# Projecting queries and keys without the heads' padding, and sending each head to its quarter by DMA

## The chip, the cores and the metric

The kernel runs on one core of a Trainium2 chip. The metric is the device time of one execution in microseconds (us). One core has TensorE (PE), VectorE (DVE), ScalarE (ACT), GpSimd (POOL) and SyncE (SP), each with its own queue of instructions in program order, and sixteen DMA engines. Transfers are issued by instructions on the queues of SP, ACT and POOL; "Lnnn" is a line of the kernel before.

## The reference

x has 4 batches of 512 tokens with 288 features; a condition of 4 x 288 steers the normalisations.

```python
mod = silu(c) @ w_adaln + b_adaln                  # six vectors of 288 for each batch
sh_msa, sc_msa, g_msa, sh_mlp, sc_mlp, g_mlp = split(mod, 6)
h = layernorm(x) * (1 + sc_msa) + sh_msa
q, k, v = heads(h @ w_qkv + b_qkv)                 # 16 heads of 18
o = softmax(q @ k.T * 18**-0.5) @ v                # per batch and head, 512 x 512
x = x + g_msa * (o @ w_proj + b_proj)
xn = layernorm(x) * (1 + sc_mlp) + sh_mlp
gates, idx = top2_softmax(xn @ w_gate)             # 4 experts, two for each token
moe = sum over the two experts e of gate * (gelu(xn @ w1[e] + b1[e]) @ w2[e] + b2[e])
x = x + g_mlp * moe                                # hidden size 1152
U = qr(P).Q                                        # 288 x 64
R = expm(A(silu(c) @ W.T + b))                     # one skew 64 x 64 matrix for each batch
out = x + ((x @ U) @ R - x @ U) @ U.T
```

All of it is float32.

## The kernel before

**Attention.** The four batches are done one after another. A batch is 4 groups g of 4 heads, a group 4 steps t of 128 keys: n = 4*b + g counts the groups, and a step (g, t) of a batch does the scores z of 4 heads (L1678: eight matmuls into two z tiles), two exps on ScalarE into es (L1687) and, one step later, the products av of es and the values vt (L1696). In the tiles each head has 32 partitions, of which 18 are used, so that z and av can take a quarter of TensorE's array for each head. The values of a batch are products pv of the transposed, modulated rows hT (L1625); VectorE adds the bias bv on the way to vt (L1632).

**Queries and keys.** The padding of a head to 32 lies already in the weights: wqk holds 4 groups x 128 columns, with zeros in the rest of each head's 32. `project(n)` makes two products for group n, one for the queries and one for the keys. Each is three matmuls (the 288 features in three chunks of 96 rows) into a bank pq, and ScalarE adds the bias on the way from pq to the group's tile qk (L1662), of which there are two by turns. No transfer is needed. There are 16 groups and so 32 products. The products of batch 0's first group stand ahead of the loop; those of group n+1 are done in the steps (g, 0) or (3, 1) and (g, 2) of group n.

**The division.** `normalize(n)` copies a group's av to oraw (ScalarE, L1715). Row 18 of each head's 32 holds the sums of the weights; four DMAs on SP's queue bring them to den (L1718), VectorE takes the reciprocals (L1724), four more bring them back into rr (L1728), and in the next group VectorE spreads them over the heads' rows as rd (L1735) and multiplies into oT (L1736). `merge` then projects oT (po, L1752) and adds the result to x (og, L1761; POOL's xs, L1762).

**What lies in the steps besides.** The code gives each step a list of pieces, in an order written by hand: `also((g, t), piece)` puts a piece at its end, and `beside` holds a queue of pieces of which each step takes one. Such pieces are:
- the modulation for the later stages (`pr`, L1200, with the weights wadb; modrows; POOL's pairs mdr, gates and modrow, L1213 and L1214), and behind it on POOL's queue the loads of the rotation's weights wr, whose results go through a DRAM tile udr (L1266, a row of stores on SP's queue) into the matrices of the exponential (pf, pw, L1335 to L1364);
- the columns of the QR (L1480 to L1525, a chain of small VectorE instructions for each of 64 columns);
- the routing of the batch before: the logits, the top two, the ranks and at last `where` (L2005), the slot of each token and expert for batches 0 and 1;
- POOL's scatters of the normalised rows into those slots (L2008): each step takes one or two from a list, 16 of them in batch 3, and the load xg of the first expert's slots is on POOL's queue behind the last of them (L2051 to L2056). TensorE's transposes for the first expert wait for xg.

**After the attention** come the experts (ph, L2296; pe, L2356) and the rotation, on which TensorE is busy to the end.

**Ahead of the loop** VectorE clears one vt (L1045, 128x2048), POOL clears the other and some constants, the first rows xs are normalised (rs on POOL, xh on VectorE), transposed (L1143), and the first products and values follow. On SP's queue stand the loads of wada, x, wqk (in two pairs), wadb and the rest; on ScalarE's those of badT, bqk, wv and bv.

**Banks.** The products pq, pv, pr, po and the transposes share three PSUM banks (`bank`), z has two tiles of two banks, av one. hT has one buffer.

Of the kernel before, what the change touches and what calls it, by code (L numbers as in the profile page):

```python
# [10 lines left out]
F32 = mybir.dt.float32  # L11
I32 = mybir.dt.int32
AF = mybir.ActivationFunctionType
# [5 lines left out]
P = 128  # L19
# [794 lines left out]
def fast_path(  # L814
# [123 lines left out]
    def bank(shape, name):  # L938

        banks[0] += 1  # L940
        if third and banks[0] % 3 == 0:
            return third[0].tile(shape, F32, tag="n", name=name)
        return ps_m.tile(shape, F32, tag="m", name=name)
# [10 lines left out]
    with ExitStack() as s1:  # L954
# [14 lines left out]
        nc.sync.dma_start(out=wada, in_=wad[:, :, : 2 * C])  # L969
        badT = const.tile([CC, 6, NK], F32, name="badT")  # L970
        nc.scalar.dma_start(out=badT, in_=b_adalnT)
        bqk = const.tile([P, 2, NG], F32, name="bqk")
        nc.scalar.dma_start(out=bqk, in_=b_qk)
        for t in range(NT):
            nc.sync.dma_start(out=xs[:, t, :], in_=x[0, ts(t, P), :])

# [2 lines left out]
        nc.gpsimd.memset(scp, 0.0)  # L979
        sc = scp[:, :, :B]  # L980
        nc.scalar.activation(sc, cs, AF.Silu)
        wqk = wat.tile([CC, NK, 2, NG * P], F32, name="wqk")
        wqv = w_qk.rearrange("(k p) t f -> p k t f", p=CC)
        for i in range(2):
            nc.sync.dma_start(out=wqk[:, :, i, :P], in_=wqv[:, :, i, :P])
        wv = wat.tile([CC, NK, C], F32, name="wv")
        nc.scalar.dma_start(out=wv, in_=w_v.rearrange("(k p) f -> p k f", p=CC))
        bv = const.tile([P, C], F32, name="bv")
        nc.scalar.dma_start(out=bv, in_=b_v.partition_broadcast(P))
        for i in range(2):  # L990
            nc.sync.dma_start(out=wqk[:, :, i, P:], in_=wqv[:, :, i, P:])
        wadb = ada.tile([CC, NK, 4 * C], F32, name="wadb")
        nc.sync.dma_start(out=wadb, in_=wad[:, :, 2 * C :])
        badr = ada.tile([P, C], F32, name="badr")
        nc.gpsimd.memset(badr, 0.0)
        for i in range(4):
            nc.sync.dma_start(
                out=badr[i * HQ : i * HQ + B, :],
                in_=b_adaln[ds((2 + i) * C, C)].partition_broadcast(B),
            )  # L1000
        pt = rot.tile([D, C], F32, name="pt")
        nc.sync.dma_start(out=pt, in_=pT)
        for b in range(1, B):
            nc.sync.dma_start(
                out=xs[:, b * NT : (b + 1) * NT, :],
                in_=x[b].rearrange("(t p) c -> p t c", p=P),
            )
        bp = const.tile([P, C], F32, name="bp")
        nc.sync.dma_start(out=bp, in_=b_proj.partition_broadcast(P))
        wgT = const.tile([CC, NK, E], F32, name="wgT")  # L1010
        nc.sync.dma_start(out=wgT, in_=w_gate)
        b1s = const.tile([P, E, NF], F32, name="b1s")
        nc.sync.dma_start(out=b1s, in_=b1T)
        nc.sync.dma_start(out=wp, in_=w_proj.rearrange("g p c -> p g c"))

        def shift_scale(between):
            pm = bank([P, 2, NK, B], "pm")
# [122 lines left out]
        def modulate_T(b, which, xh, k, dst):  # L1140
            pt = bank([P, N], f"pt{which}{b}{k}")
            for t in range(NT):
                nc.tensor.transpose(  # L1143
                    pt[:CC, ts(t, P)], xh[:, t, ds(k * CC, CC)], ident
                )
            nc.scalar.activation(
                dst[:, k, :],
                pt[:CC, :],
                AF.Identity,
                bias=modT[:, 2 * which, k, b : b + 1],  # L1150
                scale=modT[:, 2 * which + 1, k, b : b + 1],
            )
# [36 lines left out]
        def other_modulation():  # L1189

            rows = ada.tile([P, C], F32, name="modrows")
            mdr = dram.tile([4, B, C], F32, name="mdr")
            to = (gates[:, 0], modrow[:, 0], modrow[:, 1], gates[:, 1])

            def product():

                pr = bank([P, N], "pr")
                for k in range(NK):
                    for i in range(4):
                        nc.tensor.matmul(  # L1200
                            pr[ts(i, HQ), :C],
                            scp[:, k, :],
                            wadb[:, k, ts(i, C)],
                            start=(k == 0),
                            stop=(k == NK - 1),
                        )
                nc.vector.tensor_add(rows, pr[:, :C], badr)
                one = rows[2 * HQ : 3 * HQ, :]
                nc.vector.tensor_scalar_add(one, one, 1.0)

            def spread():
                for i in range(4):
                    nc.gpsimd.dma_start(out=mdr[i], in_=rows[i * HQ : i * HQ + B, :])  # L1213
                    nc.gpsimd.dma_start(out=to[i], in_=mdr[i].partition_broadcast(P))  # L1214

            return [product, spread]

        def skew_matrices(between):
# [7 lines left out]
            udr = dram.tile([D, B, D], F32, name="udr")  # L1226
            wr = skew.tile([CC, NK, NV], F32, name="wr")
            brs = skew.tile([P, width], F32, name="brs")
            row = skew.tile([P, width], F32, name="row")

            def loads():
                for i in range(4):
# [373 lines left out]
                + [half, whole],  # L1606
            )

        hTs, oTs, qks, avs, xhs = {}, {}, {}, {}, {}
        
        def begin(b):


            xhs[b] = statistics(b, 0)
            hT = a2.tile([CC, NK, N], F32, tag="hT", name=f"hT{b}", bufs=1)
            hTs[b] = hT
            vt = vts[b % 2]

            def norm():
                xhs[b] = normalized(b, 0, *xhs[b])  # L1620

            def values(t):
                pv = bank([P, C], f"pv{b}{t}")
                for k in range(NK):
                    nc.tensor.matmul(  # L1625
                        pv,
                        hT[:, k, ts(t, P)],
                        wv[:, k, :],
                        start=(k == 0),
                        stop=(k == NK - 1),  # L1630
                    )
                nc.vector.tensor_tensor(  # L1632
                    vt[:, t, :, 0:HD],
                    pv.rearrange("p (h d) -> p h d", d=HD),
                    bv.rearrange("p (h d) -> p h d", d=HD),
                    ALU.add,
                )

            return (
                norm,  # L1640
                [lambda k=k: modulate_T(b, 0, xhs[b], k, hT) for k in range(NK)],
                [lambda t=t: values(t) for t in range(NT)],
            )

        def project(n):

            b, g = divmod(n, NG)
            qk = a2.tile([P, 2, N], F32, tag="qk", name=f"qk{n}")
            qks[n] = qk

            def product(i):
                hT = hTs[b]
                pq = bank([P, N], f"pq{n}{i}")
                for k in range(NK):
                    nc.tensor.matmul(  # L1655
                        pq,
                        wqk[:, k, i, ts(g, P)],
                        hT[:, k, :],
                        start=(k == 0),
                        stop=(k == NK - 1),  # L1660
                    )
                nc.scalar.activation(  # L1662
                    qk[:, i, :], pq, AF.Identity, bias=bqk[:, i, g : g + 1]
                )

            return [lambda i=i: product(i) for i in range(2)]

        def weigh(n, t):  # L1670


            qk, es = qks[n], []
            zs = [
                ps_s.tile([P, 2, N], F32, tag="z", name=f"z{n}{t}{i}") for i in range(2)
            ]
            for c in range(4):
                nc.tensor.matmul(  # L1678
                    zs[c // 2][:, c % 2, :],
                    qk[ts(c, HQ), 1, ts(t, P)],  # L1680
                    qk[ts(c, HQ), 0, :],
                    start=True,
                    stop=True,
                )
            for i, z in enumerate(zs):
                e = ex.tile([P, 2, N], F32, tag="es", name=f"es{n}{t}{i}")
                nc.scalar.activation(e, z, AF.Exp, scale=SCALE)  # L1687
                es.append(e)
            return es
# [14 lines left out]
        def normalize(n):  # L1704
# [26 lines left out]
                    )  # L1731

            def divide():
                rd = rt.tile([P, N], F32, tag="rd", name=f"rd{n}")
                nc.vector.stream_shuffle(rd, rr, [HD] * HQ)  # L1735
                nc.vector.tensor_mul(oTs[b][:, g, :], oraw, rd)  # L1736

            return first, reciprocals, divide

# [293 lines left out]
        NN = B * NG  # L2033
        norm, turns, values = begin(0)
        shift_scale(norm)
        for piece in turns + project(0) + values:
            piece()
        ST = CAPS[0] // P
        NB = 2
# [132 lines left out]
        for n in range(NN):  # L2172
            b, g = divmod(n, NG)
            if g == 0:
# [19 lines left out]
                for step in ((0, 0), (0, 1), (0, 3), (3, 1)):  # L2194
                    also(step, column)
                also((2, 3), lambda b=b: residual(b))
            if n + 1 < NN:
                query, key = project(n + 1)
                steps[g, int(g == 3)].insert(0, query)
                steps[g, 2].append(key)  # L2200
            if n == NN - 1:
                wx = wxs[0]
                weights = [expert_weights(0)]
# [464 lines left out]
```

## Time and profile before

| | us |
|---|---|
| median of 3 runs (732.49 to 734.12) | 732.83 |
| the profiled execution | 733.85 |
| its span in the profile | 732.1 |
| first z of batch 0, 1, 2, 3 | 26.68, 98.88, 180.64, 263.92 |
| first ph of the experts | 338.24 |

The profile comes from one execution, and its times count from the start of the span. In a row of groups stand the line, the engine, the operation, out<-in with the shapes and the number of instructions, then the busy time and the mean duration in ns of one, then the engine's idle time before them and what ended most of it. A row of the timeline has the start, the busy time, the engine, line and instructions, and in brackets the idle time ahead of it and its releaser; consecutive instructions of one kind are put together (x8). A window row gives, for a stretch of time, the busy time of each engine and in brackets its number of instructions, then the granted TensorE clock, the share of the DMA engines and GB/s. A line of the waits has the total, the number of waits and the longest.

### The profile page before, as it was taken

The page shows a single profiled execution, that of the slowest core. Times are in us where ns is not written, and L with a number is a line of the kernel's source. Part 1 is how long each engine was busy: PE and PEld are TensorE (multiplying, and loading weights), DVE is VectorE, ACT ScalarE, POOL GpSimd, SP SyncE. Part 2 cuts the span into 40 slices and gives each one's busy share as a digit, 9 for nine tenths or more (in the row PEclk, how much of TensorE's full clock was granted, in tenths as well). Part 3 has the DMA queues.
Part 4 walks back from the last instruction along what each step waited for, and adds up shares of the span by engine and source line. Part 5 has one row for each costly group of instructions (what it writes and reads, how often), then busy time and mean ns, then how long its engine had stood idle before and what let it go on. Part 6 is the DMA issues. An engine that isn't in the chain of part 4 may idle for free. (4 is left out here: it accounts for less than half of the span.)

```text
span 732.1 us, 11398 instructions
## 1 busy us (share of the span) xinstructions
PE 704.6 (96%) x3627; PEld 404.2 (55%) x3627; DVE 509.2 (70%) x2237; ACT 278.5 (38%) x427; POOL 216.9 (30%) x311
## 2 busy tenths in 40 slices
PE   6999999999999999998999999999999999999995
PEld 5432334334353444324677776777667776676763
DVE  3565678796887879685268888888888886004335
ACT  2455554454525543474222423223233232221232
POOL 4035900620026013761047064441203123031110
PEclk9999999999999999999999999999999999999998
DMA  9547700000000001144252252365324153205044
GB/s 228 149 132 196 271 3 6 1 2 2 2 1 1 3 18 60 35 147 93 61 171 70 78 179 80 131 166 165 83 77 140 28 170 78 81 29 187 37 137 146
DMA packets 65511, 66.69 MB, mean 91 GB/s; under 512 B 31625, under 2 KB 55982, under 8 KB 65441
## 3 DMA queue, kind: packets, MB, share of 16 engines
q1 hardware_dynamic: 57376, 42.48, 21.0%
q0 software_dynamic: 7360, 22.91, 9.7%
q10 hardware_dynamic: 704, 0.49, 0.3%
q8 instruction: 30, 0.49, 0.3%
q14 instruction: 41, 0.33, 0.2%
HBM read 48.08 MB, written 18.09 MB: 90 GB/s over the span
## 5 line engine op out<-in xcount | busy, mean ns | idle before, releaser
L2356 PE MATMUL pe<-w2s,hm 128*128 128x288 f32 (+1 forms) x648 | 163.7, 408 | 0.0
L1687 ACT ACTIVATE es<-z 128x1024 f32<-128x1024 f32 x128 | 124.2, 1021 | 84.6 <-PE z L1678 84.0
L2296 PE MATMUL ph<-xgT,w1s 128*128 128x288 f32 (+2 forms) x576 | 151.8, 413 | 0.4
L2356 PEld LDWEIGHTS pe<-w2s,hm 128*128 128x128 f32 (+1 forms) x648 | 118.7, 187 | 31.5 <-issue 2.3
L2296 PEld LDWEIGHTS ph<-xgT,w1s 128*128 128x128 f32 x576 | 105.8, 190 | 40.2 <-issue 11.2
L2318 ACT ACTIVATE hm<-ph,b1r 128x576 f32<-128x576 f32 (+2 forms) x72 | 49.8, 737 | 131.1 <-PE ph L2309 121.2
L1678 PE MATMUL z<-qk 32*128 32x512 f32 x512 | 90.0, 640 | 3.0 <-ACT es L1687 2.8
L1655 PE MATMUL pq<-hT,wqk 96*128 96x512 f32 x192 | 90.7, 609 | 0.0
L1696 PE MATMUL av<-es,vt 128*32 128x512 f32 x512 | 69.1, 612 | 0.0
L1655 PEld LDWEIGHTS pq<-hT,wqk 96*128 96x128 f32 x192 | 34.3, 191 | 54.1 <-issue 39.4
L2371 POOL TENSOR_TENSOR y<-y,gb 128x288 f32<-128x288 f32 x32 | 27.3, 854 | 117.6 <-ACT y L2370 117.5
L2008 POOL DMA_INDIRECT slots<-xr,where x32 | 32.0, 1001 | 92.3 <-DVE where L2005 48.6
L2370 ACT ACTIVATE y<-pe,weight 128x288 f32<-128x288 f32 x32 | 16.0, 500 | 104.8 <-PE pe L2356 104.5
L2372 POOL DMA_INDIRECT chosen<-y,place x36 | 36.6, 1017 | 57.2 <-DVE y L2368 35.0
L1678 PEld LDWEIGHTS z<-qk 32*128 32x128 f32 x512 | 25.8, 182 | 48.4 <-ACT es L1687 30.7
L1762 POOL TENSOR_TENSOR xs<-xs,og 128x288 f32<-128x288 f32 x16 | 12.6, 801 | 125.8 <-DVE og L1761 125.8
L1478 DVE SCALAR_TENSOR_TENSOR q<-q 64x1 f32<-64x1 f32 (+1 forms) x192 | 44.2, 230 | 7.0
L1662 ACT ACTIVATE qk<-pq,bqk 128x512 f32<-128x512 f32 x32 | 22.0, 687 | 69.8 <-PE pq L1655 69.8
L1489 DVE STREAM_SHUFFLE wj<-pt 32x288 f32<-32x288 f32 (+47 forms) x96 | 42.1, 439 | 0.7
L1696 PEld LDWEIGHTS av<-es,vt 128*32 128x32 f32 x512 | 10.1, 108 | 48.1 <-issue 42.7
L1752 PE MATMUL po<-wp,oT 128*128 128x288 f32 x128 | 33.8, 412 | 1.2 <-DVE oT L1736 0.7
L1460 DVE SCALAR_TENSOR_TENSOR pt<-wj,uf,pt 64x288 f32<-64x288 f32 (+62 forms) x63 | 32.6, 517 | 2.2
(273 smaller groups left out, 901.5 us busy)
## 6 DMA issues: line engine op xcount, KB each, us to landing
w2s<-in_w_dram SPq DMA_DIRECT2D x8, 1296.0 KB
w1s<-in_w_dram SPq DMA_DIRECT2D x8, 1152.0 KB
slots<-empty POOLq DMA_DIRECT2D x36, 148.0 KB
yc<-chosen SPq DMA_DIRECT2D x4, 576.0 KB
out_dram<-xs SPq DMA_DIRECT2D x8, 288.0 KB
wr<-in_wrT_dram POOLq DMA_DIRECT2D x4, 567.0 KB
xg<-slots SPq DMA_DIRECT2D x4, 512.0 KB
xg<-slots SPq DMA_DIRECT2D x3, 640.0 KB
```

The source lines that it names most:

```text
L1460: nc.vector.scalar_tensor_tensor(m, w, u[rows, :], m, ALU.mult, ALU.add)
L1478: nc.vector.scalar_tensor_tensor(s, u, part, s, ALU.mult, ALU.add)
L1489: nc.vector.stream_shuffle(wj[o : o + HQ, j:], pt[o0 : o0 + HQ, j:], [j % HQ] * HQ)
L1655: nc.tensor.matmul(pq, wqk[:, k, i, ts(g, P)], hT[:, k, :], start=(k == 0), stop=(k == NK - 1),)
L1678: nc.tensor.matmul(zs[c // 2][:, c % 2, :], qk[ts(c, HQ), 1, ts(t, P)], qk[ts(c, HQ), 0, :], start=True, stop=True,)
L1687: nc.scalar.activation(e, z, AF.Exp, scale=SCALE)
L1696: nc.tensor.matmul(avs[n][ts(c, HQ), :], vts[b % 2][:, t, 4 * g + c, :], es[c // 2][:, c % 2, :], start=(t == 0), stop=(t == NT - 1),)
L1752: nc.tensor.matmul(po, oTs[b][:, g, ts(t, P)], wp[:, g, :], start=(g == 0), stop=(g == NG - 1),)
L2296: nc.tensor.matmul(ph[:, j, :SB], w1s[:, k, ts(f, P)], xgT[:, k, ts(j, SB)], start=(k == 0), stop=False,)
L2318: nc.scalar.activation(hm[:, f, : CAPS[r]].rearrange("p (j s) -> p j s", j=NB), ph[:, :, :SB], AF.Gelu_apprx_tanh, bias=b1r[:, h, r, f : f ...
L2356: nc.tensor.matmul(po[ts(m, rows), :], slots_[:, f, :], w[:, f, :], start=(f == 0), stop=(f == NF - 1),)
L2372: nc.gpsimd.indirect_dma_start(out=chosen[h], out_offset=bass.IndirectOffsetOnAxis(ap=place[:, t : t + 1], axis=0), in_=y, in_offset=None, ...
```

## The change

The padding is taken out of the products. The 16 heads are cut into 7 + 7 + 2: `parts_of` gives five items, the queries and the keys of heads 0 to 6 (126 columns each), of heads 7 to 13 (126 each), and queries and keys of heads 14 and 15 together (72). A batch thus has 5 products, where it had 8. `compact` builds the weights without padding from the loaded ones, on ScalarE: one large copy and some copies of a single row for each item. The row is the bias: the weights get a 97th row in their first chunk, hT a 97th row of ones, so that the eviction is a copy. The values get their bias in the same way, and their eviction moves from VectorE to ScalarE.

The result of a product is not where z reads it: a head's 18 rows must be at its quarter. So the evictions go to `row` (one buffer) or `last`, and `send` brings each head from there to the tile of its group by a DMA on ScalarE's queue: one of 18x1024 for q and k of a head, for heads 14 and 15 two of 18x512. That is 18 transfers for a batch. The four qk tiles now live as long as the kernel; VectorE clears them once (128x1024 each), since only 18 of each 32 rows are ever written.

The order: heads 0 to 6 of batch 0 are projected and sent ahead of the loop, before the values. In the loop a batch projects heads 7 to 13 in steps (0,0) and (0,1) and sends them in (0,2) to (1,1), projects heads 14 and 15 in (0,3) and sends them in (1,2) and (1,3). In (3,0) and (3,1) heads 0 to 6 of the next batch are projected, four are sent in (3,2) and three in (3,3).

With it come some moves: wadb takes the space of the padded weights `raw`, so its load and all later loads (`late_loads`) are issued behind the compacts; pt is loaded on ScalarE's queue; bqk, the broadcast of bv and the tile rd are gone; in the rotation's part `row` is the tile brs.

```diff
-        for i in range(2):
-            nc.sync.dma_start(out=wqk[:, :, i, :P], in_=wqv[:, :, i, :P])
...
+        HS = 7
+        wqk = wat.tile([CC + 1, NK, 5, HS * HD], F32, name="wqk")
+        raw = ada.tile([CC + 1, NK, 4 * C], F32, tag="raw", name="raw")
+        rawq = raw[:CC, :, : 2 * NG * P].rearrange("p k (t f) -> p k t f", t=2)
+        for at, n in ((0, HS * HQ), (HS * HQ, (NH - HS) * HQ)):
+            for i in range(2):
+                nc.sync.dma_start(out=rawq[:, :, i, ds(at, n)], in_=wqv[:, :, i, ds(at, n)])
...
+        def parts_of(item):
+            if item < 4:
+                return [(0, item % 2, item // 2 * HS, HS)]
+            return [(0, 0, 2 * HS, 2), (2, 1, 2 * HS, 2)]
...
+        def compact(item):
+            w = wqk[:CC, :, item, :].rearrange("p k (h d) -> p k h d", d=HD)
+            for at, i, h, n in parts_of(item):
+                nc.scalar.copy(
+                    w[:, :, ds(at, n), :],
+                    rawq.rearrange("p k t (h r) -> p k t h r", r=HQ)[:, :, i, ds(h, n), :HD],
+                )
...
+            for at, i, g, c, n in in_groups(item):
+                nc.scalar.copy(w[:, ds(at, n), :], b[:, i, g, ds(c, n), :HD])
+        qks = []
+        for g in range(NG):
+            qk = wat.tile([P, 2, N], F32, name=f"qk{g}")
+            nc.vector.memset(qk, 0.0)
+            qks.append(qk)
...
+            nc.gpsimd.memset(hT[CC : CC + 1, 0, :], 1.0)
...
-                nc.vector.tensor_tensor(
-                    vt[:, t, :, 0:HD],
...
+                nc.scalar.copy(vt[:, t, :, 0:HD], pv.rearrange("p (h d) -> p h d", d=HD))
...
-                nc.scalar.activation(
-                    qk[:, i, :], pq, AF.Identity, bias=bqk[:, i, g : g + 1]
-                )
...
+                nc.scalar.copy(row[:n, i, :], pq[:n])
+
+            def send(h):
+                qk, c = qks[h // 4], h % 4
+                if part < 2:
+                    nc.scalar.dma_start(
+                        out=qk[ds(c * HQ, HD)], in_=row[ds((h - HS * part) * HD, HD)]
+                    )
+                    return
+                for i in range(2):
+                    nc.scalar.dma_start(
+                        out=qk[ds(c * HQ, HD), i, :],
+                        in_=row[ds((2 * i + h - 2 * HS) * HD, HD), 0, :],
+                    )
...
-                rd = rt.tile([P, N], F32, tag="rd", name=f"rd{n}")
-                nc.vector.stream_shuffle(rd, rr, [HD] * HQ)
-                nc.vector.tensor_mul(oTs[b][:, g, :], oraw, rd)
+                o = oTs[b][:, g, :]
+                nc.vector.stream_shuffle(o, rr, [HD] * HQ)
+                nc.vector.tensor_mul(o, oraw, o)
...
-        for piece in turns + project(0) + values:
+        compact(0)
+        compact(1)
+        for piece in turns:
+            piece()
+        products, sends = project(0, 0)
+        for piece in products + sends:
+            piece()
+        for item in range(2, 5):
+            compact(item)
+        wadb = ada.tile([CC + 1, NK, 4 * C], F32, tag="raw", name="wadb")
+        nc.sync.dma_start(out=wadb[:CC], in_=wad[:, :, 2 * C :])
+        late_loads()
+        for piece in values:
             piece()
...
-            if n + 1 < NN:
-                query, key = project(n + 1)
-                steps[g, int(g == 3)].insert(0, query)
-                steps[g, 2].append(key)
+            if g == 0:
+                products, sends = project(b, 1)
+                also((0, 0), products[0])
+                also((0, 1), products[1])
+                also((0, 2), *sends[:2])
+                also((0, 3), *sends[2:4])
+                also((1, 0), *sends[4:6])
+                also((1, 1), *sends[6:])
+                products, sends = project(b, 2)
+                also((0, 3), *products)
+                also((1, 2), sends[0])
+                also((1, 3), sends[1])
+            if g == 3 and b + 1 < B:
+                products, sends = project(b + 1, 0)
+                also((3, 0), products[0])
+                also((3, 1), products[1])
+                also((3, 2), *sends[:4])
+                also((3, 3), *sends[4:])
```

## The prediction

> **What bounds the kernel now.** I read the slices and the groups first, then the busy time by batch, then the program order of the engines around every step of the change.
>
> ```profile
> PE   6999999999999999998999999999999999999995
> L1655 PE MATMUL pq<-hT,wqk 96*128 96x512 f32 x192 | 90.7, 609 | 0.0
> L1662 ACT ACTIVATE qk<-pq,bqk 128x512 f32<-128x512 f32 x32 | 22.0, 687 | 69.8 <-PE pq L1655 69.8
> L1687 ACT ACTIVATE es<-z 128x1024 f32<-128x1024 f32 x128 | 124.2, 1021 | 84.6 <-PE z L1678 84.0
> ```
>
> TensorE is busy nearly everywhere, the 32 products of queries and keys take 90.7 us of it, and ScalarE idles waiting for TensorE. On this view alone fewer products are pure gain. The windows of the four batches (each starts at its first z) correct that; the columns are PE, PEld, DVE, ACT, POOL:
>
> ```profile
> 26.70:98.90 72.20, 70.78 (x387) 24.23 (x386) 48.56 (x217) 40.00 (x46) 36.72 (x64) 1.00 0.51 158
> 98.90:180.60 81.70, 77.74 (x403) 30.70 (x402) 64.96 (x278) 40.57 (x48) 16.08 (x21) 1.00 0.02 3
> 180.60:263.90 83.30, 81.48 (x455) 34.23 (x454) 67.81 (x279) 40.47 (x48) 16.16 (x21) 1.00 0.01 2
> 263.90:333.00 69.10, 66.36 (x367) 25.29 (x370) 58.04 (x251) 35.32 (x41) 36.52 (x41) 1.00 0.25 73
> ```
>
> Only batch 2 is filled by TensorE (81.48 of 83.30). Batches 0, 1 and 3 have other chains close beneath it. I take them in turn below.
>
> **What goes.** 12 of 32 products. One product is three matmuls and takes 2.77 us (the pair at 36.11 hands over at 38.88), so TensorE has 33.2 us less work: 3 products, 8.3 us, in each batch's loop (8, 8, 8, 6 become 5, 5, 5, 3; the two ahead of the loop stay). The rest of TensorE's work, the 399 us after 333 included, is untouched.
>
> **The front, +5.2.** VectorE gets four memsets of 128x1024. Its 128x2048 one took 1.76, so half of that each, 3.5 in all, ahead of the vt memset for which POOL waits (1.31 now). POOL's memsets end at 12.2 instead of 8.7, rs follows them, xh goes from 10.58 to about 13.9. TensorE had the second half of pm until 12.85 anyway, so pq starts about 1.8 late, at 17.1, and ends at 22.7; copies to 23.3. Now ScalarE has 7 sends queued before anything else: its own DMA issues at the start took 0.34 to 0.45, so 7 x 0.40 = 2.8 (bounds 2.4 and 4.3, the latter from SP's 2.44 for four den). Then the compacts of items 2 to 4: two of 378 elements at 0.55 (COPYs of 384 took 0.47, 512 took 0.59), two short ones at 0.30 (192 took 0.31), eight of one row at 0.2 (the smallest ACT copies took 0.19): 3.3. So the first vt copy begins at 29.4, where VectorE's add ran at 22.42. Three banks hold pv, so the fourth pv waits until 29.9, takes 1.45, and z comes at 31.4 to 31.9 instead of 26.68. I take +5.2; the table load (1.28), now behind the vt copies, puts the first exp no earlier than that. Range 4 to 7.5.
>
> **The mod product, +8.1.** Now pr runs behind one product, then behind two:
>
> ```profile
> 27.75 2.84 PE L1655 MATMUL pq<-hT,wqk 96*128 96x512 f32 x6
> 32.47 1.64 PE L1200 MATMUL pr<-wadb,scp 96*32 96x288 f32 x24
> 36.11 2.84 PE L1655 MATMUL pq<-hT,wqk 96*128 96x512 f32 x6
> ```
>
> 5.2 + 2.77 puts it at 40.5. Its load, put behind the compacts on SP's queue, issues at about 29.4; 1296 KB at the 228 GB/s of the first slice is 6 us, so it is there at 36 and costs nothing. From pr hangs a chain: modrows, POOL's pairs to 51.3, the four wr loads (567 KB each, issued at 52.13 to 54.2, landed 59.6 to 66.3). Among them run the four rr of the first group (issued 51.80 on), which land in 4 to 8 us instead of the 1.7 of a quiet stretch:
>
> ```profile
> DVE rd L1735 <- DMA rr<-den: 21.9, 8, 10.2
> ```
>
> The 10.2 is VectorE at rd of the first group, 62.18. In the new order wr moves by 8.1, and the first den and rr move by 5.2 plus one product earlier in the group, 8.0: they meet again. So rd goes to about 70.3, and all of VectorE's reflector columns behind it are 8.1 late.
>
> **The sends of batch 1, +12 at its start.** They stand on ScalarE's queue in step (3,2), ahead of the exps of (3,3). In the compiled order, SP's and ScalarE's transfers share eight semaphores in turn, so a send waits on ScalarE until the transfer eight places before it has landed. For these four it is SP's rr of group 2:
>
> ```profile
> 95.92 0.50 DVE L1460 SCALAR_TENSOR_TENSOR pt<-wj,uf,pt 64x282 f32<-64x282 f32 x1
> 96.35 0.24 DVE L1724 RECIPROCAL den<-den 128x16 f32<-128x16 f32 x1
> ```
> ```profile
> 96.62 3.36 SPq L1728 DMA_DIRECT2D rr<-den  x4
> 100.02 4.93 SPq L1266 DMA_DIRECT2D udr<-row  x13
> ```
>
> SP already waits for VectorE here: step (3,2) began at 87.05, the reciprocal came behind a column at 96.35. With 8.1 added it is 104.5, rr goes out at 104.7 to 108 and lands 1.7 later; the four sends get away by about 110, and only then do the exps of (3,3) free the z banks: batch 1 begins at about 111 instead of 98.9, though TensorE alone would have reached it at 98.9 + 5.2 - 8.3 = 95.8.
>
> [...] If ScalarE paid only its 0.40 an issue, the start would be the 95.8 above.
>
> **Batch 1, -1.** VectorE runs without a gap from 101.12 to 145 (four columns, divides, squarings), and TensorE waits on it at 122.09 for oT (0.73), at 145.07 (0.92), 154.16 (0.79) and 160.93 (0.82). Three products taken from between let it arrive earlier at the same waits. What VectorE loses is four adds to vt, 4 x 0.46. Bounds 0 and -6 (if the last third goes back to TensorE); I take -1, by those waits.
>
> **Batch 2, -6.5.** TensorE fills it, so the 8.3 counts, less some 2 for sends that hold exps. Sum at `where`, 3.6 us into batch 3: 12 - 1 - 6.5 = +4.5, of which I take 4 (267.5 becomes 271.5).
>
> **Batch 3, nothing.** The end hangs on POOL's 16 scatters, each waiting for the one before to land, then on the xg load:
>
> ```profile
> 267.56 1.13 POOL L2008 DMA_INDIRECT slots<-xr,where  x1 [33.54 <-DVE where L2005]
> 270.97 0.98 POOL L2008 DMA_INDIRECT slots<-xr,where  x1 [2.28 <-DMA slots<-xr,where]
> 273.72 0.97 POOL L2008 DMA_INDIRECT slots<-xr,where  x1 [1.77 <-DMA slots<-xr,where]
> ...
> 317.90 1.21 POOL L2008 DMA_INDIRECT slots<-xr,where  x1 [2.19 <-DMA slots<-xr,where]
> 321.24 0.94 POOL L2051 DMA_DIRECT2D xg<-slots  x1 [2.13 <-DMA slots<-xr,where]
> ```
>
> From `where` to xg landed at 331.8 it is 64.3 us with no TensorE in it; its last 8.3 saved buy idle time. The experts then start where they start now, plus 4.
>
> **Costed at nothing.** ScalarE's sum: 12 evictions fewer at 0.69 and 20 cheaper by 0.1 (a COPY of 512 takes 0.59) is -10.2; 16 copies to vt at 0.47 and 72 sends at 0.40 are +36. Spread over four batches that is 6.5 each, against 32 us that ScalarE idles in every window; what costs is where they wait, counted above. The ones row of hT (POOL, ahead of a batch's norm), rd shuffled into oT, row kept in the tile of brs and pt on ScalarE's queue change no transfer or engine that something waits for; were POOL's memset not covered, it costs at most its 1.05 of rs once a batch.
>
> Sum: the profiled execution is 733.85 (span 732.1 and 1.75 around it), so 737.9; it lay 1.0 above the median of 732.83, so the median to expect is 736.8.
>
> **Rivals.** *The first rr gets ahead of wr* (the other side, 0.20). Each is issued about 0.3 us from the other today. If in the new order the last of the four rr goes out before the first wr, by about 2 us, they land in 1.7; rd then comes at about 63 instead of 70.3, the +8.1 on VectorE is gone, batch 1 starts at about 103, and `where` ends 2 to 4 early: 729 to 731. For it: the reciprocal at 51.49 needs only den, while wr needs POOL's pairs. Against: both moved by the same 8 us in my sum.
> *The saving goes through* (0.07): sends never wait long, VectorE follows. Batches 0 to 2 give 3 x 8.3 = 24.9, less 5.2 in front: 713. The even gaps on VectorE in batch 2 speak for it, the waits of batch 1 against.
> *Near zero* (0.13): the delay of VectorE is half of what I count, or batch 1 gives 4 to 5.
> *Sends cost more* (0.15): 0.61 each as SP's den, and waits on slots in batches 1 and 2 as well: 18 x 0.2 = 3.7 a batch, 741 to 745.
> The forecast itself has 0.45, at 735 to 740.
>
> Range 727 to 745: it leaves out the saving that goes through and the worst of dear sends. No change means within 0.2%, 1.5 us, about what a measurement of this kernel can tell. Faster is 0.20 + 0.07 = 0.27, same 0.13, slower 0.45 + 0.15 = 0.60.
>
> **What would show it.** First z at 31 to 33; pr near 40; rd of the first group near 70; ScalarE idle ahead of the four sends of (3,2) with rr of group 2 just landing; batch 1 from about 111, batch 2 shorter than 78, `where` at 271 and 64 us from it to xg. If batch 1 begins before 104 the slot waits are not there, and the first rival holds; if the stretch from `where` to xg shrinks, my claim that batch 3 gives nothing is wrong.

## The result and the profile after

The changed kernel takes 758.06 us (median of 4 runs, 756.10 to 762.34), the kernel before 732.66 in the runs beside it: a ratio of 1.035 with a 95% interval of 1.030 to 1.040. The forecast had been 736.8, within 727 to 745: slower, but by 4 us and not by 25. The profiled execution took 756.10, its span 754.4.

The page of the changed kernel has the slices of TensorE, the products and the exps as follows. From here on, the L number of a row is a line of the kernel that the row comes from.

```profile
PE   5798796968999699994999999999999999999994
L1749 ACT ACTIVATE es<-z 128x1024 f32<-128x1024 f32 x128 | 124.1, 1021 | 107.9 <-PE z L1740 79.7
L1702 PE MATMUL pq<-hT,wqk 96*126 96x512 f32 (+3 forms) x120 | 59.1, 631 | 0.0
```

The products shrank from 90.7 us to 59.1, about as counted. But TensorE, almost without a gap before, now has holes in the first half, and ScalarE's idle time ahead of the exps grew from 84.6 to 107.9. A matmul of a product takes 631 ns on average and took 609: something slows TensorE itself. The windows of the four batches, from first z to first z (the last to 356), with the granted clock in the column before the last two:

```profile
38.00:122.90 84.90, 70.12 (x366) 23.87 (x366) 46.46 (x211) 39.11 (x47) 37.26 (x65) 0.90 0.60 180
122.90:205.20 82.30, 72.81 (x384) 28.56 (x384) 60.47 (x263) 40.59 (x51) 16.63 (x22) 0.93 0.08 17
205.20:288.00 82.80, 75.24 (x437) 32.60 (x436) 64.83 (x266) 39.57 (x49) 16.63 (x22) 0.94 0.07 16
288.00:356.00 68.00, 57.93 (x349) 22.69 (x352) 57.06 (x251) 33.39 (x41) 36.28 (x41) 0.92 0.30 87
```

The first z came 11.4 us late, batch 0 took 12.7 longer than before, batches 1 and 2 as long as before (82.3 and 82.8, against 81.7 and 83.3). So everything was lost before batch 1 began, at 122.9 instead of 98.88, and almost nothing was won back (the first ph of the experts came at 361.4 instead of 338.24). And the clock, 1.00 in all four windows before, is 0.90 to 0.94. The front as TensorE saw it:

```profile
34.85 3.25 PE L1672 MATMUL pv<-wv,hT 97*128 97x288 f32 x6 [5.33 <-ACT vt L1679]
38.03 2.09 PE L1740 MATMUL z<-qk 32*128 32x512 f32 x8
40.05 3.74 PE L1702 MATMUL pq<-hT,wqk 97*126 97x512 f32 x6
```
```profile
29.50:34.80 5.30, 0.02 (x1) 0.00 (x0) 0.00 (x0) 3.46 (x14) 0.00 (x0) 0.70 0.21 56
34.80:38.00 3.20, 3.15 (x6) 1.85 (x6) 0.00 (x0) 0.61 (x3) 0.00 (x0) 0.50 0.75 177
```

The fourth pv waits 5.33 us for ScalarE. Then it takes 3.25 instead of 1.45, the first z 2.09 instead of 1.14, the product 3.74 instead of 2.84: the granted clock behind the idle stretch is 0.50. The start of batch 1, on ScalarE, TensorE and SP:

```profile
116.94 4.83 ACTq L1714 DMA_DIRECT2D qk<-row  x4
121.82 1.02 ACT L1749 ACTIVATE es<-z 128x1024 f32<-128x1024 f32 x1 [10.77 <-DMA qk<-row]
122.90 2.99 PE L1740 MATMUL z<-qk 32*128 32x512 f32 x8 [7.11 <-ACT es L1749]
```
```profile
113.04 2.44 SPq L1790 DMA_DIRECT2D rr<-den  x4
115.52 5.46 SPq L1310 DMA_DIRECT2D udr<-brs  x13
128.24 2.44 SPq L1780 DMA_DIRECT2D den<-oraw  x4
130.73 8.93 SPq L1310 DMA_DIRECT2D udr<-brs  x23
139.76 2.84 SPq L1790 DMA_DIRECT2D rr<-den  x4
```

The exp of (3,3) waits 10.77 us behind four sends, and TensorE 7.11 us for the exps. The first send goes out at 116.94, 1.4 us after SP began the 13 stores to udr that stand behind rr. The second goes out at 119.52, 2.1 us after SP issued the store that used its semaphore before it (117.41; all transfers of SP and ScalarE share eight semaphores in this trace); the third and fourth follow at once. The last row matters too: the rr of group 3 goes out at 139.76 though its reciprocal was done at 132.3, because 23 stores stand ahead of it. In the kernel before, the den of group 3 was out by 107.5, the stores ran while VectorE worked towards its reciprocal, and rr went out 1.2 us behind it (116.04).

### The profile page after: what moved, and what is told of

Read it like the earlier page. It is cut to its first block, busy times and chain, and to the rows that moved or that the text cites. A ratio compares the mean times of both kernels' runs of the same rounds, so it can differ in the third digit from the quotient of the medians.

```text
span 754.4 us, 11370 instructions
## 1 busy us (share of the span) xinstructions
PE 686.4 (91%) x3555; PEld 397.2 (53%) x3555; DVE 508.8 (67%) x2225; ACT 278.9 (37%) x449; POOL 218.1 (29%) x315
## 5 line engine op out<-in xcount | busy, mean ns | idle before, releaser
L1749 ACT ACTIVATE es<-z 128x1024 f32<-128x1024 f32 x128 | 124.1, 1021 | 107.9 <-PE z L1740 79.7
L1740 PE MATMUL z<-qk 32*128 32x512 f32 x512 | 94.7, 686 | 10.4 <-ACT es L1749 10.2
L1758 PE MATMUL av<-es,vt 128*32 128x512 f32 x512 | 72.3, 639 | 0.0
L1702 PE MATMUL pq<-hT,wqk 96*126 96x512 f32 (+3 forms) x120 | 59.1, 631 | 0.0
L1740 PEld LDWEIGHTS z<-qk 32*128 32x128 f32 x512 | 28.8, 196 | 55.0 <-ACT es L1749 38.1
L1702 PEld LDWEIGHTS pq<-hT,wqk 96*126 96x126 f32 (+3 forms) x120 | 21.7, 192 | 36.7 <-issue 33.5
L1672 PE MATMUL pv<-wv,hT 96*128 96x288 f32 (+1 forms) x96 | 29.3, 451 | 6.0 <-ACT vt L1679 5.3
```

The costliest lines, as they stand in the source:

```text
L1702: nc.tensor.matmul(pq[:n], wqk[:rows, k, item, :n], hT[:rows, k, :], start=(k == 0), stop=(k == NK - 1),)
L1740: nc.tensor.matmul(zs[c // 2][:, c % 2, :], qk[ts(c, HQ), 1, ts(t, P)], qk[ts(c, HQ), 0, :], start=True, stop=True,)
L1758: nc.tensor.matmul(avs[n][ts(c, HQ), :], vts[b % 2][:, t, 4 * g + c, :], es[c // 2][:, c % 2, :], start=(t == 0), stop=(t == NT - 1),)
```

## The experiments

**Where the loss arises: the front and the sends in the loop.** First the seven sends ahead of the loop were moved to SP (`project` gets the queue for `send` as an argument), then the rest of the front was repaired: the last compacts were put ahead of the first products, and the memsets of the qk tiles behind that of vt.

```diff
-        products, sends = project(0, 0)
+        products, sends = project(0, 0, nc.sync)
```

> The changed kernel, with the seven sends ahead of the loop issued by SP and not by ScalarE. Theory A (a late front is handed on whole by VectorE's chain, and ends in batch 1's start): ScalarE gets back 5.4 us, the fourth pv no longer waits 5.3 us, TensorE keeps its full clock, so the first z comes at about 31 instead of 38.0 and the execution ends 10 to 14 us earlier, at about 745. Theory B (the sends inside the loop set the end by themselves): first z at 31 too, but at most 3 us off the end, 755 or more.

Measured: 746.63 us (743.09 to 748.78), ratio 1.020 (1.016 to 1.023); first z at 29.46, batch 1 at 108.78.

```diff
+        for item in range(2, 5):
+            compact(item)
         products, sends = project(0, 0, nc.sync)
...
             vts.append(vt)
+        qks = []
+        for g in range(NG):
+            qk = wat.tile([P, 2, N], F32, name=f"qk{g}")
+            nc.vector.memset(qk, 0.0)
+            qks.append(qk)
```

> As the run before, and besides the compacts of items 2 to 4 ahead of the first products (ScalarE idles there) and VectorE's memsets of the qk tiles behind that of vt. Theory A: first z near 27, batch 1 from 102 to 108, the execution at 733 to 741. Theory B: first z near 27, the execution still at 750 or more.

Measured: 744.27 us (741.38 to 745.72), ratio 1.016 (1.012 to 1.020); first z at 27.76, batch 1 at 106.41. Theory A holds in the main: one late stretch of 11 us on ScalarE ahead of the loop was worth 11 to 14 us at the end. But it is not all: the 733 to 741 expected of the second run are missed, and 12 us are left. The next two runs leave sends out, so their results are not the reference's.

```diff
-                also((3, 2), *sends[:4])
-                also((3, 3), *sends[4:])
```

> The changed kernel without the seven sends in steps (3,2) and (3,3): the next batch's heads 0 to 6 are still projected and copied, but batches 1 to 3 use those of batch 0. If the wait of these sends for SP's rr of group 2 holds ScalarE (10.8 us at batch 1), batch 1 begins at 113 to 117 instead of 122.9, and the execution takes 748 to 751. If VectorE's lateness sets the end by itself, batch 1 begins earlier too, but the execution stays within 2 us of 757.

Measured: 751.69 us (749.46 to 756.88), ratio 1.027 (1.021 to 1.033); first z at 37.19, batch 1 at 114.23. The time is just above the expected 748 to 751. The sends ahead of batches 1 to 3 cost the whole execution 6 us; ahead of batch 1 alone ScalarE had waited 10.77 us for them and TensorE 7.11.

> The repaired front (sends ahead of the loop on SP, compacts earlier, memsets later), and no sends at all inside the loop: all batches use the q and k that batch 0's first transfers brought, heads 7 to 15 use zeros, so only the time counts. If the sends inside the loop cost what is left over the kernel before, it takes 727 to 733; if VectorE's chain or the late mod product does, it stays within 3 us of the repaired front's 744.

Measured: 736.55 us (730.45 to 739.99, 10 runs), ratio 1.0041 (1.0007 to 1.0075). The sends in the loop are worth 7.7 us on top of the repaired front. The forecast of 727 to 733 is missed, though: with no send in the loop, and 12 products less, it is still 3 to 4 us behind the kernel before.

**What holds the sends.** The repaired front, with the stores to udr issued by POOL, and then all sends on SP besides.

```diff
             def stores(i, half):
...
-                        nc.sync.dma_start(
+                        nc.gpsimd.dma_start(
                             out=udr[r, :, ds(r + 1 + lo - at, hi - lo)],
```

> The repaired front, and the 63 rows stored to udr issued by POOL instead of SP. The sends of batch 1 then no longer wait for stores queued behind SP's rr, and the rr of group 3 no longer stands behind 23 stores. If these queues are the cause, batch 1 begins at 99 to 102 instead of 106.4, the rd of group 3 comes 5 to 8 us earlier, and the execution takes 733 to 739. If ScalarE's own issues (18 x 0.73 us a batch) are the cause, it stays at 742 or more.

> As the run before, and the sends inside the loop issued by SP too, so that no transfer stands ahead of the exps on ScalarE's queue. If the products that are gone are worth something once nothing holds the exps, it is the fastest of these, 728 to 734; if SP's queue now delays rr and den by its 18 x 0.75 us a batch, it is no faster than the run before.

Measured: 746.33 us (743.29 to 749.79), ratio 1.017 (1.014 to 1.021), and 746.06 us (742.65 to 751.92), ratio 1.017 (1.013 to 1.021). By their times both fall on the second of the two alternatives, but they don't decide between them: POOL now issues the 66 stores in one piece of 33.85 us, and the merge's additions queue behind it (VectorE's og waited 7.28 us for POOL's xs). What the first run does show is that the sends no longer wait: they go out as soon as ScalarE reaches them, and the exp of (3,3) waits 2.73 us instead of the 8.23 of the repaired front. The second does not say what ScalarE's own time for the issues is worth, for on SP's queue the seven sends take 5.68 us among den and rr. So the stores were left out, but for those of the first row.

```diff
-                    if lo < hi and count % 2 == half:
+                    if lo < hi and count % 2 == half and r == 0:
```

> The repaired front (744.3 us) with the stores to udr left out but for those of its first row (the matrices of the exponential are then zero there, so only the time counts). SP's queue holds only den and rr, and no send has to wait for a store. If the stores behind SP's rr are what holds ScalarE ahead of batch 1, the sends go out at about 98 and batch 1 begins at 100 to 103 instead of 106.4, the rd of group 3 comes at 117 to 121 instead of 127.9, and the execution takes 736 to 741. If it is the sends' own issues and landings, batch 1 begins at 105 or later and the execution stays above 742.

Measured: 737.43 us (734.49 to 738.22, 7 runs), ratio 1.0053 (1.0023 to 1.0083), against 744.27 with the stores. ScalarE at the same place, in the repaired front and then without the stores:

```profile
100.83 4.46 ACTq L1714 DMA_DIRECT2D qk<-row  x4
105.34 1.02 ACT L1749 ACTIVATE es<-z 128x1024 f32<-128x1024 f32 x1 [8.23 <-DMA qk<-row]
```
```profile
103.29 3.03 ACTq L1714 DMA_DIRECT2D qk<-row  x4
106.36 1.94 ACT L1749 ACTIVATE es<-z 128x1024 f32<-128x1024 f32 x2 [2.73 <-DMA qk<-row]
```

The four sends go out as soon as ScalarE reaches them and take 0.76 each; the exp waits 2.73 instead of 8.23, and VectorE's wait for the rr of group 3 (6.15) is gone. Batch 1 itself did not begin earlier (108.30 against 106.41), so that part of the expectation failed (and the division of group 3 came at 122.8, not at 117 to 121): in this execution TensorE ran at a clock of 0.50 from 72.6 to 86.2, behind two waits of 1.0 and 1.5 us, and its 24 matmuls with wr (pa) ended at 81.8 instead of 77.2. What was gained came in batch 1, 79.8 us instead of 84.9. So it is the stores, more than the issues, that made the sends dear. How their 6.8 us divide between the wait of the sends and that for the rr of group 3 is not separated.

**The half clock.** Matmuls are repeated where TensorE idles; they add work and take away only the idling.

```diff
+                turns_ = {(0, 2): 4, (1, 3): 5}.get((b, t), 1)
-                for k in range(NK):
+                for k in list(range(NK)) * turns_:
```

> The changed kernel with matmuls repeated where TensorE idles: the third pv of batch 0 is computed four times (4.4 us of the 5.3 us wait ahead of the fourth), the last pv of batch 1 five times (5.8 us of the 7.1 us wait ahead of batch 1). They add work and remove only the idling. If the half clock after an idle stretch costs time, the fourth pv takes 1.5 instead of 3.25, the first z 1.1 instead of 2.1, pr comes at 44 to 45 instead of 48.6, and the execution is 3 to 7 us shorter, 750 to 754. If the halved clock falls on time that is waiting anyway, it stays within 1.5 us of 757.

Measured: 750.53 us (747.90 to 753.90), ratio 1.024 (1.019 to 1.029): three products of pv more in the one idle stretch, four in the other, and 7 us less time. The fourth pv took 1.72 us instead of 3.25, the first z 1.14 instead of 2.09, and pr came at 44.32 instead of 48.56.

**What the products are worth at all.** The kernel before, with 12 products taken out and nothing put in (its scores are then not the reference's).

```diff
             def product(i):
+                if i == 1 and g > 0:
+                    return
...
-                    qk[ts(c, HQ), 1, ts(t, P)],
+                    qk[ts(c, HQ), int(n % NG == 0), ts(t, P)],
```

> The kernel before, with the product of the keys left out in groups 1 to 3 of each batch (z takes the queries for both, so the scores are not the reference's): 12 products fewer, 33.2 us less work for TensorE, and nothing else changed, no sends and no new front. If TensorE's saving went through up to batch 3 it would take 708 to 712; if VectorE's chain and the scatters take it up, as the forecast had it, 722 to 731.

Measured: 730.97 us (729.74 to 735.51, 10 runs), ratio 0.9984 (0.9966 to 1.0003): 33.2 us less work on an engine that is busy 96% of the time, and no difference that this measurement can tell from none. It lies at the upper end of what VectorE's chain and the scatters would give. Its TensorE in batch 1, and the same window in this kernel and in the one before:

```profile
139.96 0.34 PE L1335 MATMUL pf<-fs,every 64*64 64x4 f32 x2 [3.70 <-POOL xr L1779]
140.23 2.09 PE L1680 MATMUL z<-qk 32*128 32x512 f32 x8
```
```profile
98.00:180.00 82.00, 74.90 (x395) 29.48 (x388) 65.06 (x285) 40.23 (x48) 16.04 (x21) 0.94 0.02 3
```
```profile
98.00:180.00 82.00, 78.04 (x404) 30.92 (x404) 64.96 (x278) 40.57 (x48) 16.08 (x21) 1.00 0.02 3
```

The first window is that with 12 products fewer, the second that of the kernel before. TensorE, relieved, arrives early at pf (a product for the matrices of the exponential), waits 3.70 us for what VectorE and POOL have not finished, and does the next z at half clock (0.50 from 140 to 144; 2.09 us instead of 1.14). Its busy time falls by 3.1 us in a window from which some 8 of work were taken: by the mean clock of 0.94 about 5 us went into slower matmuls (6% of 82, an estimate). Three runs took this apart.

```diff
                 pf = bank([P, N], "pf")
+                for _ in range(8):
+                    nc.tensor.matmul(pf[:, :C], ident, wp[:, 0, :], start=True, stop=True)
```

> The kernel with 12 products fewer, and matmuls put into its three longest waits for VectorE in batches 1 and 2 (8 x 0.41 us ahead of pf, which waited 3.70; 6 ahead of the first po of batch 1's merge, 2.75; 8 ahead of the first psq, 3.69). They do nothing but keep TensorE from idling. If the half clock behind these waits gives the saving back, the clock stays at 1 through batches 1 and 2 and the execution takes 2 to 5 us less than the 731.0 without filling. If VectorE's chain alone holds the end, it stays within 1 us of 731.0.

Measured: 729.20 us (727.52 to 731.29, 10 runs), ratio 0.9947 (0.9928 to 0.9967). Useless matmuls in three waits (the third at psq, the first squaring of the exponential) bring 1.8 us by the medians, 2.7 by the ratios, about the low end of the 2 to 5 expected; the clock of that window is 0.98 and of batch 2's 1.00. It did not stay at 1 throughout: the next wait, at pw (3.41), took pf's place.

```diff
             def column(j):
+                if j in (8, 9, 13, 14):
+                    return
```

> The kernel with 12 products fewer, and four of the QR's columns left out, two in batch 1 and two in batch 2 (5.5 to 6 us of VectorE each, 23 us in all). If TensorE and VectorE hold each other, so that either saving alone is worth next to nothing, this takes 716 to 724; if something else holds the end (the transfers, the clock), it stays within 3 us of 731.0.

> The kernel before, all products, with the same four columns left out. If TensorE is the closer bound there, as the slices say, this takes 729 to 732.5; if VectorE alone was the bound of batches 1 and 2, 715 to 724.

Measured: 725.40 us (724.48 to 727.53, 6 runs), ratio 0.9900 (0.9877 to 0.9924), with products and columns less; 731.78 us (729.23 to 732.95, 12 runs), ratio 0.9979 (0.9964 to 0.9993), with the columns less alone. VectorE's busy time fell by 18.5 us in the second (509.2 to 490.7), less than the 23 expected. So 33 us off TensorE alone bring 0.2%, some 20 us off VectorE alone 0.2%, both together 1.0%. The two engines hold each other. Why both together bring only 7.8 us and not the 9 to 17 expected is not shown: the half clock is still there in that run (0.94 and 0.96 in batches 1 and 2), and a third chain may lie beneath.

**All repairs together.** The repaired front, with its waits ahead of batch 1, pf and psq filled by matmuls (14, 14 and two more turns of a pv).

> All of the change with the repaired front (744.3 us), and matmuls put into its three longest waits of TensorE: 14 x 0.41 us ahead of pf (waited 6.49), 14 ahead of the first psq (6.65), the last pv of batch 1 computed three times (2.9 of the 4.56 us ahead of batch 1). If the half clock behind the waits is most of what is still lost, it takes 735 to 739; if the sends and VectorE hold the end whatever the clock, 742 or more. By what was measured for the products (1.6 us) it is not faster than the kernel before in either case.

Measured: 739.00 us (737.74 to 743.31, 6 runs), ratio 1.011 (1.008 to 1.014), 5.3 us less than without the filling; the clock is 0.98 in batch 1 and 1.00 in batch 2. It is the fastest of the runs that keep the whole change, and it doesn't beat the kernel before. Nor did free sends without the filling (736.55); the two together were not run.

## Why the prediction was right and wrong

It was right on the sign, and on where: a late front, the mod product and with it VectorE's columns later, ScalarE held by the sends of (3,2), nothing from batch 3. It was wrong on the size, 25 us instead of 4, by three terms and one misreading.

**The front: +5.2 became +11.4.** The failed term is ScalarE's price of a send. I took 0.40 us from its loads at the start and 0.61 as the upper end; seven sends took 5.42, 0.77 each (SP needs as long: 5.50 for the same seven). Another 2.3 came from the first products, which started 1.2 late against the forecast and took 6.7 us for 5.65: the first four of their matmuls took 0.89 to 1.06 each, the rest 0.59, and the clock's record in this trace begins only at 21.41, just as they end (in the kernel before at 15.94, behind one such matmul). And one term the sum did not have: the wait of the fourth pv, which I had seen coming, brought the clock to 0.50 from 31.65 to 41.89 (pv +1.8, and after it z +1.0, product +0.9).

**The mod product: +8.1 became +16.1** (32.47 to 48.56), made of 11.4, one product of 2.8 and the 1.9 of half clock on z and product. The rest of this step held: the load of wadb, issued at 34.40, cost nothing, and rr met wr again (VectorE waited 11.1 us at the first division).

**The sends of batch 1: +12 became +24.** The place was right and the wait measured (10.77). What they wait for was named one transfer short: not rr itself but the stores behind it on SP's queue. The first and the second send waited for a store each (issued at 115.52 and 117.41; the sends went out at 116.94 and 119.52), so that four took 4.83 us where without the stores they took 3.03. And rr was 16 late by the steps above, not 8. That the stores would also get ahead of the rr of group 3, once its den comes late, I had not seen at all; the run without stores shows both gone.

**Batch 1, -1: measured +0.6**, just outside the bounds of 0 and -6. The reading that TensorE there waits for VectorE was right (6.5 us at pf in the changed kernel). That VectorE runs there without a gap was not: in the kernel before it waits for TensorE's po, 0.81 us at 129.09 and 1.48 at 131.03.

**Batch 2, -6.5: measured -0.5.** This is the misreading. "TensorE fills it" was taken from 81.48 busy of 83.30, and the 8.3 us counted at full worth. The share alone didn't say that: batch 0 was as full (70.78 of 72.20). The run with nothing but the products taken out shows them to be worth at most about 1.6 us in the whole kernel; its batch 2 was even longer (85.7). VectorE's chain lay directly beneath, and what TensorE saved in front of it was idled and then lost again to the half clock (the mean clock from 180 to 262 was 0.94 in that run, 1.00 in the kernel before). The same holds for the rival in which the saving goes through: there never were 24.9 us to be had.

**Batch 3, nothing: right.** From the first scatter to xg it took 53.68 us before, from 267.56 to 321.24, and now 53.62:

```profile
289.58 1.13 POOL L2070 DMA_INDIRECT slots<-xr,where  x1 [32.91 <-DVE where L2067]
...
343.20 0.93 POOL L2125 DMA_DIRECT2D xg<-slots  x1 [2.10 <-PE z L1740]
```

The rest of the kernel, from the first ph to the end of the span, was untouched (393.9 us before, 393.0 after).

**The rivals.** That the first rr gets ahead of wr didn't happen in the changed kernel. It did in the run with 12 products fewer: rr went out at 49.55, wr at 53.06, and the division came at 53.84 instead of 62.18. The condition was stated rightly, but VectorE being 8 us early in batch 0, with 33 us of products less besides, left 1.6 us at the end, so its price of 2 to 4 looks too high. "Sends cost more" was the rival nearest to the truth: the issues cost more than its 0.61 each. Its waits on slots in later batches hardly show (the four sends ahead of batch 2 go out 0.76 apart, from 199.62 to 201.90), and its sum, 741 to 745, lacked the clock and the stores.

How the 25 us split, by the ratios: the front 14 (1.035 to 1.016), the sends in the loop 8 to 9 (to 1.004), the rest 3. What that rest is was not isolated; in that run TensorE still waits 6.4 us at pf and 6.6 at psq, and runs at 0.92 and 0.94 in batches 1 and 2. Filling such waits in the repaired front with its sends brought 5 us.

## What to carry to other kernels

An engine that is busy 96% of the time is not thereby the bound: take work from it alone, leaving everything else, before paying for the saving with transfers. Here that one run would have shown 1.6 us for 33. When a step puts transfers on the queue of an engine that others wait for, look up what the transfer's semaphores were used for last, and on which queue that stands: four sends took 4.83 us behind stores of a quite different stage, on another engine's queue, and 3.03 without them. And a wait that one creates on TensorE is to be counted with what may follow it at half clock: here waits of 1.86 to 7.11 us went with 3.41 to 10.24 us at 0.50.

## What the runs showed of the hardware

The granted clock fell to 0.50 in or behind waits of TensorE of very different lengths: 7.11 us (ahead of batch 1 in the changed kernel, 0.50 from 120.40 to 127.22), 2.75 (ahead of a po at 199.90 in the run with fewer products), and in the kernel before, near the end of its attention, 1.86:

```profile
331.91 0.63 PE L2090 MATMUL pt<-ident,xg 128*128 128x128 f32 x4 [1.86 <-DMA xg<-slots]
```
```profile
332.00:334.00 2.00, 2.00 (x16) 0.81 (x20) 1.72 (x9) 0.69 (x4) 0.00 (x0) 0.85 0.00 0
334.00:336.00 2.00, 2.00 (x11) 0.49 (x4) 1.74 (x11) 2.00 (x4) 0.00 (x0) 0.50 0.00 0
```

In the run without the stores it fell behind two waits of 1.0 and 1.5 us, 1.0 apart. How long a wait must be for this was not shown. Behind the wait of 2.75 the clock stayed at 0.50 for 3.42 us (200.55 to 203.97), behind that of 1.86 for 3.41 (333.38 to 336.80); in the run without the stores it stayed for 13.7 (72.56 to 86.21), though TensorE was busy from 74.66 on. Ahead of the experts, the half-clock stretches of the changed kernel lasted 10.24, 3.41, 6.83, 6.83, 6.83, 10.24 and 13.65 us, each a whole multiple of 3.41; in the run with fewer products, by windows of 2 us, about 3.4, 6.8, 3.4, 3.4 and 6.8. The duration of a product went from 2.84 to 3.74, that of a group of z from 1.14 to 2.09.

The 12 products more thus did something: with them, in the kernel before, TensorE's clock was 1.00 from 15.94, where its record begins, to 333.38 us; without them and with nothing else changed it fell five times before 262 us. Repeated matmuls that no one reads made three different kernels faster, by 7, 5 and 2 us.
